# Two transformer layers with experts: dense pieces placed between and behind double score steps, and another order of pieces between layer 0's attention and the experts

## The chip, the cores and the metric

The kernel runs on one core of one Trainium2 chip. The metric is the time of one execution in device microseconds, lower is better; it is given as the median of repeated runs. All engines of the core work side by side: TensorE (PE in the profile, with its weight loads as PEld), VectorE (DVE), ScalarE (ACT), GpSimd (POOL) and SyncE (SP, which here only issues DMAs). Each engine runs its own instructions in the order in which the program wrote them, and waits on semaphores for the others.

## The reference

The input is `x` of 8 images, 1024 tokens, 256 features, all in fp32. Four blocks follow each other, each on the layer norm of `x` and added to `x`:

```python
x = x + _L0_attn_ref(_layernorm(x), ...)   # 16 heads of 16, a window of 128 tokens to each side
x = x + _L0_ffn_ref(_layernorm(x), ...)    # 8 experts, the best 2 per token, and a shared expert
x = x + _L1_attn_ref(_layernorm(x), ...)   # 16 heads, blocks of 64: own band, first and last block
x = x + _L1_ffn_ref(_layernorm(x), ...)    # one product with a ternary weight, and a bias
```

In layer 0's feed-forward each token goes through the two experts with the largest logits, weighed by a softmax of the two, and through the shared expert. An expert is `silu(x @ wg.T) * (x @ wu.T) @ w_down.T` with 384 hidden features. In layer 1's attention the first and the last block of 64 queries see all 1024 keys; the others see the first and the last block and the three around them.

## The kernel before

The program has three stretches: layer 0's attention over images 0 to 7, the experts over groups of 256 or 128 gathered tokens, and layer 1's attention over images 0 to 7. What else has to be done (norms, projections, routing, the shared expert, the last product) is cut into small **pieces** that are put beside the attention.

**Steps.** `attention` (used by both layers) walks through steps. A step writes, in this order: `weights` (the products of keys and queries for one pack of key tiles, 4 heads side by side in 4 PSUM banks, line 459; ScalarE takes the exponential of each bank, line 466, and in layer 0 POOL cuts the window's edge out of it, line 915); `sums` of the pack of two steps ago (line 489, all into one bank); one call of `scores` (the same products the other way round, four banks, line 404; VectorE takes each bank's row maximum, lines 422, 427 and 431); whatever is `later` (transposes of maxima, line 442, or of a finished sum, line 504); and then pieces. Scores run ahead of weights, since the maximum is put into the queries before the weights are made. There are 7 PSUM banks for all of this but the sums. Layer 0 has 24 steps for an image and 32 score rounds, layer 1 has 28 steps and 36 rounds. So some steps call `scores` twice, the **double steps**: in layer 1 those are steps 2, 6, 9, 13, 16, 20, 23 and 27 of an image. In such a step pieces can stand between the two calls and behind the second.

```python
if some:
    fill_until(step + 0.5)
    scores(*some.pop(0))
fill_until(step + 1)
```

**Due times.** `beside` holds, for each image, lists of pieces with due times in steps, counted from the image's step 0. `fill_until(time)` runs all pieces that are due before `time`, the earliest first. So a piece with a due time of 9.3 stands between the two calls of step 9, one of 9.8 behind them. A list given with one start and one end time spreads its pieces over that time by their weights. Times of 28 and more fall in the next image's steps. `need` can draw a piece forward when something requires it.

**Pieces of layer 1.** For image b: `qk_pieces` (eight products for queries and keys, two matmuls each on TensorE at line 282, then activations on ScalarE, lines 302 and 314), the first four heads' pairs as `first` in the image before, the others in the image's own steps; `values` (two matmuls, line 338, and a VectorE add, in `v_pieces`); `gather` (an indirect DMA by POOL) and `add` for the experts' outputs; `stats`, `scaled` (norm; `scaled` also holds the transposes, line 235). For image b-1, which has just left the attention: `stats`, `scaled`, `biased` (POOL), and eight `product` pieces (line 1324: two matmuls, a VectorE add, and a store on SP after every second one).

**Pieces at the end of layer 0.** When attention works on image 7, it has beside it the projection, norm and routing of image 6. `route_pieces` are `logits`, `by_token`, two `best` (VectorE's top 8), `mine`, `counts` (two matmuls at line 721 that wait for `mine`, then some 14 small VectorE operations) and `weighed`; after them come 16 `scatter` pieces, each a small POOL copy and an indirect DMA (lines 742 and 751) that put rows in their experts' buckets in DRAM. Behind image 7's attention stands one `chain` of pieces, in a fixed order: image 7's projection (line 878, after transposes at line 867), norm, routing and scatter; the tables that say which expert each group belongs to (`ranges`, `rests`, `offsets`, `groups`, all on VectorE, and `by_group`, line 1114, a matmul with VectorE behind it); and the shared expert of image 6, cut into 12 `up` pieces (8 matmuls in the profile's count at line 611, a tanh at line 617, two VectorE operations at lines 622 and 623) and 4 `down` pieces (line 631, with an add at line 795). `some(n)` takes the next n pieces of the shared expert. Two `up` pieces can be taken in two parts, `shared_in_two`: the matmuls and the tanh, and later the VectorE part, `gated`.

**The experts.** `experts` loads for each group the rows (`xs`, line 1160, only after the last scatters) and the expert's weights (lines 1172 and 1174) by tables that `by_group` made: SP reads `which` and `where` and issues the loads.

Of the kernel before, what the change touches and what calls it, by code (L numbers as in the profile page):

```python
# [19 lines left out]
B, S, D = 8, 1024, 256  # L20
# [30 lines left out]
def seq_kernel(  # L51
# [135 lines left out]
    def piece(weight, f, *args, first=(), then=None):  # L187
        return weight, lambda: f(*args), first, then
# [582 lines left out]
    shared_in_two = {}  # L771
# [35 lines left out]
    def layer0():  # L807
# [42 lines left out]
        def before_it(b):  # L850
            qk_of[b], xnT_of[b] = {}, []
            norm = norm_pieces(b, "xnT", xnT_of[b], "xnT")
            first = qk_pieces(b, 0, 0, wq_sb, wk_sb, xnT_of[b], qk_of[b])
            values = v_pieces(b, 0, wv_sb, xnT_of[b])
            return norm, first, [
                piece(0.1, biased, b, jp, first=[("xnT", b, 3)]) for jp in range(4)
            ], values
# [84 lines left out]
        for b in range(B + 1):  # L942
            lists = []
            if b == 0:
                (stats, scaled), first, biases, values = before_it(0)
                lists.append((-1, -1e-6, (
                    stats + scaled[:2] + [piece(0.0, f) for f in (clear_maxima, masks)] + scaled[2:]
                    + first + [piece(0.0, ones_in_v, 0)] + values + biases
                )))
                lists.append((1, 2, [piece(0.0, clear_bucket), piece(0.0, ones_in_v, 1)]))  # L950
            if b > 0:
                half0, half1, (stats, scaled), route, scatter, shared = after_it(b - 1)
            if b < B:


                lists.append((
                    0, [4.7, 5.3, 5.8, 6.6],
                    qk_pieces(b, 1, 0, wq_sb, wk_sb, xnT_of[b], qk_of[b]),
                ))
                if b > 0:  # L960
                    lists.append((0, [-0.1, -0.05, 0.6, 1.6], half0))
                    lists.append((0, [2.7, 2.75, 3.5, 4.3], half1))
                    lists.append((0, [3.1, 4.1, 4.8, 7.2], stats))
                    lists.append((0, [6.1, 6.8, 8.85, 10.2, 10.7], scaled))
                    if b + 1 < B:
                        lists.append((0, [11.7, 12.5, 13.6, 15.5, 16.3, 16.8, 18.1], route))
                        lists.append((0, [17 + 0.8 * i for i in range(STREAMS)], scatter))
                    else:
                        lists.append((11.3, 14, route))
                        lists.append((14, 20.5, scatter[:10]))  # L970
                    late = scatter[10:]
            if b == B:

                def some(n):
                    return [rest.pop(0) for _ in range(n)]

                ranges, rests, offsets, groups, by_group = tables()
                lists.append((0, [0.1] * 6, late))

                lists.append((0, [1.1] * 2 + [2.05] * 3, half0[:3] + stats[:1] + half0[3:]))  # L980
                two = [shared_in_two[B - 2](*x) for x in ((0, 2), (1, 0))]
                chain = (
                    stats[1:2] + half1[:3] + scaled[:1] + stats[2:3] + half1[3:] + stats[3:]
                    + scaled[1:2] + some(1) + scaled[2:3] + some(1) + scaled[3:] + route[:5]
                    + [x[0] for x in two] + route[5:6] + scatter[:4] + [x[1] for x in two]
                )
                some(2)
                chain += (
                    some(1) + [ranges] + some(1) + [rests] + some(1) + [offsets] + some(1)
                    + [groups] + some(3) + [by_group] + scatter[4:] + route[6:] + rest  # L990
                )
                lists.append((2.1, 8, chain))
                left_over.extend(shared)
            elif b + 1 < B:


                if b > 0:
                    lists.append((
                        0, [7.6, 8.3, 8.7, 9.6, 10.6, 11.3, 11.8, 12.6, 13.5, 14.3, 14.8, 15.6]
                        + [20.3, 23.4, 26.3, 26.8, 26.85], shared,  # L1000
                    ))
                (stats, scaled), first, biases, values = before_it(b + 1)
                lists.append((0, [2.9 if b > 1 else 0.0], [piece(0.0, load, b + 1)]))
                lists.append((0, [7.8, 9.8, 12.1, 12.8], stats))
                lists.append((0, [13.1, 13.8, 15.1, 15.8, 16.2], scaled))
                lists.append((0, [16.7, 17.3, 17.8, 18.6], first))
                lists.append((0, [19.5, 20.8, 21.6, 22.6], values))
                lists.append((0, [18.5, 20.5, 21.8, 23.5], biases))
            else:

                rest = shared
            beside.append(lists)
# [216 lines left out]
    def layer1():  # L1229
# [174 lines left out]
        for b in range(B + 1):  # L1404
            lists = []
            if b == 0:
                (gather, add), (stats, scaled), first, values = before_it(0)

                rest = [piece(x[0], x[1]) for x in left_over]

                def some(n):
                    return [rest.pop(0) for _ in range(n)]

                begun = gather[:]
                for j, n in enumerate((3, 2, 1, 2, 1, 2, 1, 1)):
                    begun += some(n) + add[j : j + 1] + (stats[j // 2 : j // 2 + 1] if j % 2 else [])
                for x in scaled:
                    begun += [x] + (some(1) if len(rest) > 1 else [])
                lists.append((-1, -1e-6, begun + first + rest))
                lists.append((-0.95, -0.1, values))  # L1420
            if b < B:
                lists.append((
                    0, [0.4, 1.4, 2.2, 3.3, 4.4, 5.4, 6.2, 7.6],
                    qk_pieces(b, 1, 1, wq_sb, wk_sb, xnT_of[b], qk_of[b]),
                ))
            if b == B:
                (stats, scaled), biases, products = after_it(b - 1)
                scaled, turned = scaled[:4], scaled[4:]
                lists.append((
                    0, [-1.9, -0.9, -0.8, -0.7, 0.9, 0.92, 0.94, 0.96, 1.8, 1.9] + [2.5] * 14,  # L1430
                    stats[:2] + scaled[:2] + turned[:1] + biases[:1] + turned[1:2] + biases[1:2]
                    + products[:4] + stats[2:] + scaled[2:] + turned[2:] + biases[2:] + products[4:],
                ))
            elif b > 0:
                (stats, scaled), biases, products = after_it(b - 1)
                lists.append((0, [1.6, 2.8, 4.6, 5.5], stats))
                lists.append((0, [5.7, 7.4, 8.4, 10.3, 11.3], scaled))
                lists.append((0, [7.9, 8.8, 10.9, 11.8], biases))
                lists.append((0, [9.7, 10.5, 11.4, 12.6, 13.2, 13.8, 14.6, 15.6], products))
            if b + 1 < B:  # L1440
                gathered, (stats, scaled), first, values = before_it(b + 1)
                if b == 0:
                    lists.extend(combining(
                        gathered, 1.5, [0.5 + 0.4 * i for i in range(16)],
                        [3.5, 4.5, 5.5, 6.8, 7.5, 8.5, 9.5, 10.3], b + 1,
                    ))

                lists.append((0, [5.6, 7.6, 10.4, 10.7] if b == 0 else [-7.1, -3.6, 0.6, 10.6], stats))
                lists.append((0, [11.5, 12.4, 14.4, 15.4, 16.4], scaled))
                lists.append((0, [16.8, 17.3, 17.7, 18.4, 19.4, 20.2, 20.7, 21.3], first))  # L1450
                lists.append((0, [19.8, 21.7, 22.3, 23.2, 24.2, 25.3, 26.3, 27.2], values))
            if b + 2 < B:
                lists.extend(combining(
                    gathers(b + 2), 16.2, [12 + 0.6 * i for i in range(16)],
                    [18.6, 19.6, 21.4, 22.5, 24.7, 25.5, 26.5, 28.3], b + 2,
                ))
            if b + 3 < B:
                lists.append((0, [3.9], [piece(0.0, placed, b + 3)]))
            beside.append(lists)
# [8 lines left out]
    with ExitStack() as ctx0:  # L1468
        layer0()
    with ExitStack() as ctx1:  # L1470
        layer1()
# [76 lines left out]
```

## Time and profile before

| what | value |
|---|---|
| median of 3 runs | 3046.15 us (3043.94 to 3050.73) |
| profiled execution | 3047.95 us |
| its span | 3046.2 us |
| mean granted TensorE clock | 0.991 |
| layer 0's attention, of the span | up to about 1167 us |
| between it and the experts' first product | about 1167 to 1235 us |
| experts | about 1235 to 1825 us |
| layer 1, one image in the middle | 146.0 us |

All durations below come from the one profiled execution. Each line of a timeline has the start in us, the time from the first start to the last end, the engine, the line of the kernel, the operation, what it writes and reads, its shape and how many instructions were merged; behind them in brackets the idle time before and what ended it. TensorE's matmuls overlap, so the time that a group costs is read from its start to the next group's start. TensorE counts as busy while a matmul that has been issued waits; such a wait shows only as a group that takes longer than the same group elsewhere. In waits, a line gives the engine and line that waited, whom it waited for, the total, the number of waits and the longest.

### The profile page before, as it was taken

The page shows a single profiled execution, that of the slowest core. Times are in us where ns is not written, and L with a number is a line of the kernel's source. Part 1 is how long each engine was busy: PE and PEld are TensorE (multiplying, and loading weights), DVE is VectorE, ACT ScalarE, POOL GpSimd, SP SyncE. Part 2 cuts the span into 40 slices and gives each one's busy share as a digit, 9 for nine tenths or more (in the row PEclk, how much of TensorE's full clock was granted, in tenths as well). Part 3 has the DMA queues.
Part 4 walks back from the last instruction along what each step waited for, and adds up shares of the span by engine and source line. Part 5 has one row for each costly group of instructions (what it writes and reads, how often), then busy time and mean ns, then how long its engine had stood idle before and what let it go on. Part 6 is the DMA issues. An engine that isn't in the chain of part 4 may idle for free. (4 is left out here: it accounts for less than half of the span.)

```text
span 3046.2 us, 81036 instructions
## 1 busy us (share of the span) xinstructions
PE 2967.0 (97%) x32684; PEld 1907.1 (63%) x32684; DVE 1896.5 (62%) x5996; ACT 1389.0 (46%) x2845; POOL 994.3 (33%) x2406
## 2 busy tenths in 40 slices
PE   8999999999999998999999998999999999999998
PEld 4455555555555545788888885555555555555554
DVE  5667676666667665344333345776767686767564
ACT  4454454444444442122222213555556555656554
POOL 4334454545453546000000011424242434243223
PEclk9999999999999999999999998999999999999998
DMA  3000101010101001666666642101010101010000
GB/s 107 2 2 16 42 17 41 19 39 19 40 22 36 24 26 46 217 208 213 230 211 213 213 147 62 35 9 52 7 57 2 57 2 57 6 54 6 12 13 19
DMA packets 109447, 198.18 MB, mean 65 GB/s; under 512 B 11152, under 2 KB 81296, under 8 KB 109072
## 3 DMA queue, kind: packets, MB, share of 16 engines
q1 hardware_dynamic: 96784, 159.43, 15.7%
q0 software_dynamic: 12288, 33.57, 3.5%
q8 instruction: 257, 4.21, 0.6%
q14 instruction: 118, 0.97, 0.1%
HBM read 139.22 MB, written 53.74 MB: 63 GB/s over the span
## 5 line engine op out<-in xcount | busy, mean ns | idle before, releaser
L466 ACT ACTIVATE w<-pst 128x512 f32<-128x512 f32 (+1 forms) x1664 | 834.7, 589 | 581.6 <-PE pst L459 560.4
L915 POOL TENSOR_SCALAR_AFFINE_SELECT w<-w 128x256 f32<-128x256 f32 x896 | 335.4, 406 | 525.1 <-ACT w L466 523.8
L427 DVE TENSOR_REDUCE maxima<-pst 128x1 f32<-128x320 f32 (+1 forms) x896 | 368.2, 473 | 215.2 <-PE pst L404 175.9
L422 DVE CUSTOM_DVE_ANT_0 junk<-pst,mask_mid 128x320 f32<-128x320 f32 x768 | 330.6, 486 | 181.1 <-PE pst L404 177.3
L489 PE MATMUL pso<-w,v 128*32 128x256 f32 (+5 forms) x6400 | 434.7, 388 | 2.1 <-ACT oT L498 2.1
L617 ACT ACTIVATE th<-pst 128x256 f32<-128x256 f32 (+1 forms) x309 | 117.0, 379 | 654.2 <-PE pst L611 622.6
L611 PE MATMUL pst<-xsT,of 128*128 128x256 f32 (+1 forms) x1704 | 383.6, 375 | 0.8 <-ACT xsT L1186 0.7
L611 PEld LDWEIGHTS pst<-xsT,of 128*128 128x128 f32 x1704 | 313.1, 191 | 40.4 <-ACT xsT L1186 0.9
L1354 POOL MEMSET w<- 64x128 f32 x768 | 151.8, 199 | 557.6 <-ACT w L466 531.5
L1283 POOL DMA_INDIRECT y<-made,from x128 | 122.2, 955 | 620.0 <-DVE h L622 587.4
L622 DVE SCALAR_TENSOR_TENSOR h<-th,pst 128x256 f32<-128x256 f32 (+1 forms) x309 | 128.2, 415 | 289.1 <-ACT th L617 281.5
L489 PEld LDWEIGHTS pso<-w,v 128*32 128x32 f32 x6400 | 157.9, 109 | 216.4 <-issue 154.8
L431 DVE TENSOR_REDUCE two<-pst 128x1 f32<-128x512 f32 x256 | 159.0, 684 | 114.1 <-PE pst L404 84.2
L631 PE MATMUL pst<-of,h 128*128 128x256 f32 x828 | 190.5, 379 | 0.0
L631 PEld LDWEIGHTS pst<-of,h 128*128 128x128 f32 x828 | 157.0, 190 | 21.2
L623 DVE TENSOR_TENSOR h<-h,pst 128x256 f32<-128x256 f32 (+1 forms) x309 | 128.3, 415 | 10.6
L211 POOL TENSOR_TENSOR rstd<-var,neg_half 128x4 f32<-128x4 f32 x64 | 67.3, 1052 | 186.8 <-DVE var L210 132.4
L1366 POOL TENSOR_TENSOR x<-x,ao 64x64 f32<-64x64 f32 (+1 forms) x192 | 78.6, 416 | 104.1 <-DVE ao L597 86.2
L206 DVE BATCH_NORM_STATS2 stats<-x 128x6 f32<-128x256 f32 x256 | 103.9, 406 | 1.2 <-POOL x L1366 0.9
L631 PE MATMUL pst<-shared_down,h 128*128 128x256 f32 x384 | 94.4, 395 | 8.6 <-issue 4.9
L1194 DVE COPY ys<-pst 128x512 f32<-128x512 f32 (+1 forms) x71 | 48.0, 676 | 84.6 <-PE pst L631 84.5
L422 DVE CUSTOM_DVE_ANT_0 junk<-pst,mask_last 128x256 f32<-128x256 f32 x128 | 46.7, 421 | 72.9 <-PE pst L404 72.9
(831 smaller groups left out, 4886.0 us busy)
## 6 DMA issues: line engine op xcount, KB each, us to landing
of<-in_w_up_dram SPq DMA_DIRECT2D x71, 768.0 KB, 4.9
of<-in_w_down_dram SPq DMA_DIRECT2D x71, 384.0 KB
xs<-bucket SPq DMA_DIRECT2D x67, 256.0 KB, 6.2
made<-ys SPq DMA_DIRECT2D x67, 256.0 KB, 2.1
x<-in_x_dram SPq DMA_DIRECT2D x32, 256.0 KB, 3.9
between<-x SPq DMA_DIRECT2D x8, 1024.0 KB
x<-between SPq DMA_DIRECT2D x32, 256.0 KB, 3.9
out_dram<-x SPq DMA_DIRECT2D x24, 256.0 KB, 3.1
```

What stands on the lines that cost most here:

```text
L422: nc.vector.tensor_tensor_reduce(out=junk[:, 0:many], in0=ps[:, 0:many], in1=mask, scale=-1.0, scalar=3e38, op0=ALU.add, op1=ALU.min, accu ...
L427: nc.vector.tensor_reduce(to[:, r, :], ps[:, 0:many], AX.X, ALU.max, negate=True)
L431: nc.vector.tensor_reduce(twos[0][:, r, n : n + 1], ps[:, 0:many], AX.X, ALU.max, negate=True)
L466: nc.scalar.activation(w[:, r, 0:n], ps[r][:, 0:n], AF.Exp)
L489: nc.tensor.matmul(columns(po[rows[r], :], to - 512 * half, many, step), lhsT=v_of[b % 2][:, kt, head : head + 32], rhs=w[:, r, n : n + many],
L611: nc.tensor.matmul(ps[:, part * GT : part * GT + n], lhsT=up_sb[:, kc, f0 : f0 + 128], rhs=xT[:, kc, :], start=(kc == 0), stop=(kc == 1),)
L622: nc.vector.scalar_tensor_tensor(h, th, 1.0, g, ALU.add, ALU.mult)
L623: nc.vector.tensor_tensor(h, h, u, ALU.mult)
L631: nc.tensor.matmul(ps[:, t * D : (t + 1) * D], lhsT=hs[fc][:, t * 128 : (t + 1) * 128], rhs=down_sb[:, fc, :], start=(fc == 0), stop=(fc = ...
L915: nc.gpsimd.affine_select(out=part, in_=part, compare_op=ALU.is_ge, fill=0.0, base=0, pattern=[[0, 2], [sign, 128]], channel_multiplier=-sign,
L1283: nc.gpsimd.indirect_dma_start(out=y, out_offset=None, in_=made[:, :], in_offset=bass.IndirectOffsetOnAxis(ap=place[b][:, n, j : j + 1], a ...
L1354: nc.gpsimd.memset(part, 0.0)
```

## The change

Only due times and the order of pieces change; no piece is added, removed or rewritten.

In layer 0, beside the attention of image 7, the routing of image 6 gets due times of its own (before: spread from 11.3 to 14), with `counts` at 15.2 instead of 13.4, and its first ten scatters are spread from 15.4 to 21.4 instead of from 14 to 20.5. In the chain behind the attention, two more `up` pieces stand ahead of image 7's routing, other two `up` pieces are taken in two parts, the first `down` stands ahead of their `gated`, and fewer pieces of the shared expert stand between the later tables.

In layer 1, query and key pieces move from steps 1 and 7 to steps 2 and 6, one `scaled` from step 8 to 7 with two `biased`, the first three `product` pieces to steps 9, 9 and 10, and all `values` pieces to later times, the last one into step 1 of the next image.

```diff
                     else:
-                        lists.append((11.3, 14, route))
-                        lists.append((14, 20.5, scatter[:10]))
+                        lists.append((0, [11.6, 12.5, 12.9, 13.4, 13.8, 15.2, 15.7], route))
+                        lists.append((15.4, 21.4, scatter[:10]))
...
-                two = [shared_in_two[B - 2](*x) for x in ((0, 2), (1, 0))]
+                two = [shared_in_two[B - 2](*x) for x in ((1, 1), (1, 2))]
                 chain = (
-                    stats[1:2] + half1[:3] + scaled[:1] + stats[2:3] + half1[3:] + stats[3:]
-                    + scaled[1:2] + some(1) + scaled[2:3] + some(1) + scaled[3:] + route[:5]
-                    + [x[0] for x in two] + route[5:6] + scatter[:4] + [x[1] for x in two]
+                    stats[1:2] + half1[:2] + some(1) + half1[2:3] + scaled[:1] + stats[2:3]
+                    + half1[3:] + stats[3:] + scaled[1:2] + some(1) + scaled[2:3] + some(1)
+                    + scaled[3:4] + some(1) + scaled[4:] + route[:5] + [x[0] for x in two]
+                    + route[5:6] + scatter[:4] + some(1) + [x[1] for x in two]
                 )
                 some(2)
                 chain += (
-                    some(1) + [ranges] + some(1) + [rests] + some(1) + [offsets] + some(1)
-                    + [groups] + some(3) + [by_group] + scatter[4:] + route[6:] + rest
+                    [ranges] + some(1) + [rests] + some(1) + [offsets] + some(1) + [groups]
+                    + some(2) + [by_group] + scatter[4:] + route[6:] + rest
                 )
...
                 lists.append((
-                    0, [0.4, 1.4, 2.2, 3.3, 4.4, 5.4, 6.2, 7.6],
+                    0, [0.4, 2.2, 2.8, 3.4, 4.4, 5.4, 6.2, 6.8],
                     qk_pieces(b, 1, 1, wq_sb, wk_sb, xnT_of[b], qk_of[b]),
                 ))
...
                 lists.append((0, [1.6, 2.8, 4.6, 5.5], stats))
-                lists.append((0, [5.7, 7.4, 8.4, 10.3, 11.3], scaled))
-                lists.append((0, [7.9, 8.8, 10.9, 11.8], biases))
-                lists.append((0, [9.7, 10.5, 11.4, 12.6, 13.2, 13.8, 14.6, 15.6], products))
+                lists.append((0, [5.7, 7.4, 7.9, 10.3, 11.3], scaled))
+                lists.append((0, [7.6, 8.4, 10.9, 11.8], biases))
+                lists.append((0, [9.3, 9.8, 10.6, 12.6, 13.2, 13.8, 14.6, 15.6], products))
...
-                lists.append((0, [16.8, 17.3, 17.7, 18.4, 19.4, 20.2, 20.7, 21.3], first))
-                lists.append((0, [19.8, 21.7, 22.3, 23.2, 24.2, 25.3, 26.3, 27.2], values))
+                lists.append((0, [16.8, 17.3, 17.8, 18.4, 19.4, 20.2, 20.8, 21.4], first))
+                lists.append((0, [22.4, 23.2, 23.8, 24.6, 26.6, 27.2, 27.8, 29.4], values))
```

## The prediction

> **What bounds the kernel now.** I read the page first. TensorE is the bound: it is busy for 97% of the span.
>
> ```profile
> PE 2967.0 (97%) x32684; PEld 1907.1 (63%) x32684; DVE 1896.5 (62%) x5996; ACT 1389.0 (46%) x2845; POOL 994.3 (33%) x2406
> ```
>
> So the change can only win idle time, half-clock time, or waits that lie inside the "busy" time. Next come TensorE's waits between 1090 and 1215 us, where layer 0's attention ends and the experts are prepared.
>
> ```profile
> PE pst L721 <- DVE sofar L727: 4.0, 2, 3.4
> PE pst L631 <- DVE h L623: 2.8, 1, 2.8
> PE pst L235 <- DVE rows__15310 L223: 2.4, 2, 1.4
> PE pst L878 <- ACT aoT L872: 2.0, 1, 2.0
> ```
>
> L721 is `counts`: one call waits 3.36 us. The table by stretches shows what follows a starved stretch. The columns are the stretch's length, the busy time of PE, PEld, DVE, ACT and POOL, the granted clock, and DMA.
>
> ```profile
> 1122.80:1126.20 3.40, 0.23 (x3) 0.00 (x0) 3.26 (x21) 0.70 (x2) 1.56 (x5) 1.00 0.00 0
> 1126.20:1133.10 6.90, 6.72 (x48) 3.28 (x48) 3.83 (x22) 1.73 (x5) 1.27 (x4) 0.51 0.01 4
> 1194.50:1197.90 3.40, 1.08 (x6) 0.63 (x5) 2.79 (x15) 0.00 (x0) 0.30 (x2) 1.00 0.00 0
> 1197.90:1201.30 3.40, 2.95 (x7) 2.41 (x8) 1.15 (x3) 0.00 (x0) 1.25 (x2) 0.50 0.11 39
> ```
>
> After the 3.36 us wait TensorE runs 6.9 us at half clock; after the 2.77 us wait, 3.4 us. A wait costs more than its length.
>
> Last, TensorE's timeline in layer 1. I take times from start to start, since the ends are modelled. The first six lines are the ends of double steps 6, 23 and 27 of one image, with nothing behind the second scores (L404), and the next step's weights (L459 x8). The last three are double step 13 of image 7, with a dense piece (L1324) behind.
>
> ```profile
> 2348.55 1.09 PE L404 MATMUL pst<-k__26876,q__26874 32*64 32x128 f32 x32
> ...
> 2349.57 2.04 PE L459 MATMUL pst<-q__26874,k__26876 32*128 32x512 f32 x8
> ...
> 2442.48 0.80 PE L404 MATMUL pst<-k__29042,q__29040 32*64 32x128 f32 x32
> 2443.21 2.23 PE L459 MATMUL pst<-q__27743,k__27745 32*128 32x512 f32 x8
> ...
> 2461.13 1.09 PE L404 MATMUL pst<-k__29042,q__29040 32*64 32x128 f32 x32
> 2462.15 2.37 PE L459 MATMUL pst<-q__29040,k__29042 32*128 32x512 f32 x8
> ...
> 2961.35 1.09 PE L404 MATMUL pst<-k__36319,q__36317 32*64 32x128 f32 x32
> 2962.37 1.13 PE L1324 MATMUL pst<-wt_sb,xnT__36840 128*128 128x256 f32 x4
> 2963.43 1.64 PE L459 MATMUL pst<-q__36317,k__36319 32*128 32x512 f32 x8
> ```
>
> The same eight matmuls take 1.97 us (2349.57 to 2351.53) after step 6, 2.16 after step 23, 2.30 after step 27, but 1.57 with the piece behind and 1.09 at the shortest (2403.70). They wait for a bank that VectorE's maxima still hold; the page calls that busy. Such waits recur in each 146 us image.
>
> **Layer 0.** The sum is made against the profiled execution's 3047.95 us.
>
> *`counts` of image 6.* It moves from step 13 (right behind two `best`, `mine`) to step 15. VectorE's pile that it waits for (busy from 1119.08 to 1126.3) is worked off in the two steps between, so 3.36 us of wait and half of 6.9 us go: -6.8. VectorE's 2.8 us of `counts` and 0.9 of `weighed` then fall between maxima; three steps (1134.12 to 1147.93, 13.8 us) hold some 8.4 us of VectorE work (16 maxima at 0.44 from start to start, 0.69 and 0.67), so a bank may be late: +0.8 (0 to 2.0). The first scatter now follows `counts` in the same step and waits on POOL for `to`, with step 16's affine selects behind it; their readers come two steps later, and POOL idled 7.5 us before 1131.83, so 0.
>
> *Its ten scatters* (a row copy of 0.2 us and a DMA_INDIRECT of 1.0 each, 1.37 per pair with the gap) move past the selects: two now land in step 20 instead of step 19. POOL works without a gap from there:
>
> ```profile
> 1158.49 0.98 POOL L751 DMA_INDIRECT bucket<-rows__14188,torow  x1 [0.16 <-issue]
> 1159.48 6.54 POOL L915 TENSOR_SCALAR_AFFINE_SELECT w<-w 128x256 f32<-128x256 f32 x18
> ```
>
> The last 14 of these 18 selects start 2.7 us later, and the last sums wait for them. The least is 0, if selects were early; the most 2.7 and a half-clock stretch of 1.7. I take +2.5, because the last sums begin at 1165.36 and the selects end at 1166.02.
>
> *Before the last `counts`* two more up pieces (8 matmuls, 1.72 us each by L611; a tanh and two DVE of 0.42) are run. They fill the 1.96 us at L878 and the 1.36 us at the fourth `rows__15310`; the 1.00, 0.46 and 0.67 us waits stay, as VectorE sets them. 3.44 - 1.96 - 1.36 gives +0.1, and the xnT copy behind a tanh 0.3: +0.4 (0 to 0.8).
>
> *Behind it.* `down` goes ahead of the two `gated`, so the 2.77 us at L631 and its 1.7 of half clock go from TensorE. But VectorE's chain from `counts` (1194.7) to `spread` holds, by its rows in the new order (`counts`, an add of `down`, two `gated`, ranges, `gated`, rests, an add, offsets, `gated`, groups), 2.8 + 0.7 + 1.7 + 2.7 + 0.8 + 0.7 + 0.7 + 2.8 + 0.8 + 2.7 = 16.4 us, against TensorE's 12.3 (two downs of 2.7, four ups of 1.72): a new wait of about 4 us at L1114. It costs nothing while another chain is longer: the last 16 scatters run on POOL from 1197.58 to 1221.38 and their packets land by 1222.5, and the experts' first rows are loaded only then. In the trace the rows were issued at 1227.23, since SP's loads behind `which` began at 1221.70, and landed at 1233.46 beside two experts' weights. Now `which` comes near 1213, the weights are issued early, the rows at about 1223.5, and land in 3.9 to 6.2 us (page, part 6): 3.7 to 6 us earlier. Against that, TensorE's signals were up to 7 us late here (matmuls ended at 1213.0, tanh at 1220.02); if this stays, the gain is 0. I take -4.0 (-6 to 0). The 4 to 6 us idle before the experts puts up to one more stretch at half clock behind it: +0.8 (0 to 1.7).
>
> The page TensorE: Matmul & The Clock Gate of the Trainium skill (Why this matters for your kernels) asks for no idle gaps over about 3 us; here a gap of 2.77 us was followed by half clock, so the row decides. By the rule that gap would cost 1.7 less.
>
> Sum: -6.8 + 0.8 + 2.5 + 0.4 - 4.0 + 0.8 = -6.3, between -13 and +2.
>
> **Layer 1, per image.** Five pieces of two products (0.96 us, 1.06 where a copy trails) leave single steps and are put at doubles, which then have one between and one behind (steps 2, 6, 9, 23, 27; 13, 16 and 20 keep theirs). Query and key pieces bring ACT work; `product` and `values` a DVE add of 0.42; `product` 1 its store on SP, where nothing is late.
>
> Added, each at 1.06 less what the next x8 weights give back. Step 6: 1.97 becomes the 1.57 of the last fence, +0.66. Step 27: 2.30 becomes 1.57, +0.33. After doubles of kind 2, 9, 16, 23 a piece behind gave 1.49 (2364.95) and 1.09 (2403.70); I take 1.3. Step 2 (1.75 now): +0.6. Step 23 (2.16): +0.3 with 0.1 for the second scores. Step 9 gets its piece between: by step 16, which has a transpose there, 4.8 us instead of 4.34, +0.4. The last `values` is due at 29.4, the next image's step 1, ahead of the sums of step 30 that would draw it forward: its add comes at 2327.05 to 2327.47 by VectorE's queue, and the sums that read it start at 2327.25: +0.2. Together +2.5. At best the waits swallow all (+0.5); at worst nothing (+5.3).
>
> Taken away, each at 0.96 less the wait that comes to light at the next weights. The nearest rows are image 7's bare steps: x24 takes 1.55 (2985.42) with only the maxima's transposes ahead, against 1.22 after step 25 now: -0.5. Step 21: x24 1.39 becomes 1.48 (2968.11): -0.8. Step 19 keeps transposes and a key piece, as step 5, whose next weights show no wait: -1.0. Step 11: x24 1.09 becomes x16's 1.50 (2358.88): -0.55. Steps 7 and 8 (a piece leaves; a transpose moves from 8 to 7): -0.5. Together -3.35 (-4.8 if no wait comes to light, -2.3 if each bares 0.5).
>
> Net -0.87 an image for images 1 to 6. Image 0 has no products before it and nothing in its step 1: -1.4; image 7 has no `values` to make: +0.7. That is -6 in all. All best ends together would be -4.3 an image, all worst +3.0; some two thirds of the way, -3 and +2, give -21 and +14.
>
> The skill's page Trainium Kernel Development and Optimization (Best Practices) says to mind PSUM pressure: packed matmuls speed up compute, not evacuation. It speaks against this half: a piece behind takes a bank itself. By it alone the wait would move, not shrink, the worst end above; the 1.57 against 1.97 to 2.30 says that about half goes.
>
> Total: -12.3, so 3035.65 by the profiled execution, whose time lies 1.8 above the median: 3034.
>
> **The rivals.** All start from 3046.15; a measurement tells a difference from none at about 0.2%, 6 us.
>
> *The waits swallow the pieces whole:* -3 an image is some -20 in layer 1, and with layer 0's -6 that is 3020. For it: step 16, where x8 has no wait left at 1.09. Against: 1.57 after step 13.
>
> *Only `counts` counts:* late signals hold the experts' start, layer 1 gains nothing: -3, 3043. For it: tanh at 1220.02.
>
> *VectorE sets the pace in layer 1 (slower):* it is busy 105.4 of 146 us, over 90% in some steps. If each added piece costs its 1.06 in full (+5.3 instead of +2.5), an image takes 1.9 us more: +14, with layer 0's -6 some 3054. It decides from +0.9 an image (no gain left), and from +1.8 the kernel is slower by 0.2%. Against: the 1.57 after step 13.
>
> **How the numbers follow.** Likeliest, as summed, 0.5 (3026 to 3040 by itself); the waits swallow all 0.17; only `counts` 0.20; VectorE 0.13. Faster gets 0.49 + 0.17 + 0.07 = 0.73; slower 0.11; within 0.2% the rest. 3017 to 3049 leaves out some 0.05 below and 0.14 above.
>
> **What would show it.** Right: no wait at `counts` of image 6 and full clock after it; a new wait of about 4 us at L1114; the first rows 4 us earlier after `counts`; x8 weights behind doubles at 1.1 to 1.6 us and images of 145 us. Wrong: a longer wait for the last sums than 3 us, x24 weights over 1.6 us after bare steps, or images over 147 us.

## The result: slower, by 0.4%

The changed kernel takes 3060.66 us, the median of 6 runs (3053.80 to 3063.30), against 3045.05 us before (6 runs, 3043.26 to 3050.73) on the same chip: a ratio of 1.004, with a 95% interval of 1.0025 to 1.0055. The forecast was 3034 us and "faster". The profiled execution took 3059.23 us, with a span of 3057.5 us, 11.3 us more than before.

In the listings of the changed kernel, and of every version with the new chain, lines behind the chain are numbered one higher than before: L1325 is `product`, L1115 `by_group`. On the profile's page TensorE's busy time has hardly moved:

```profile
PE 2968.1 (97%) x32684; PEld 1900.7 (62%) x32684; DVE 1895.2 (62%) x5996; ACT 1387.3 (45%) x2845; POOL 994.7 (33%) x2406
```

The waits of TensorE say where the time went. First the longest line of the kernel before, which the forecast did not show (total, number of waits, longest):

```profile
PE pst L235 <- DVE xn L223: 25.5, 9, 9.7
```

and the same view of the changed kernel:

```profile
PE pst L235 <- DVE xn L223: 42.9, 16, 9.2
...
PE pst L1115 <- DVE spread L1106: 4.1, 1, 4.1
...
PE pst L721 <- DVE sofar L727: 3.2, 6, 0.5
```

The 3.36 us wait at `counts` (L721) is gone, and `by_group` waits 4.1 us, as forecast. But the transposes of layer 1's `scaled` (L235) wait seven times more, 17.4 us in all. Here is one of the seven, in TensorE's timeline:

```profile
2352.06 1.13 PE L282 MATMUL pst<-xnT__26517,wk_sb 128*128 128x256 f32 x4
2353.12 1.31 PE L459 MATMUL pst<-q__26874,k__26876 32*128 32x512 f32 x8
2354.37 1.08 PE L489 MATMUL pso<-w,v 128*32 128x256 f32 x24
2355.37 1.11 PE L404 MATMUL pst<-k__26876,q__26874 32*64 32x512 f32 x16
2356.42 0.66 PE L235 MATMUL pst<-ident,xn 128*128 128x128 f32 x4
2359.69 1.09 PE L235 MATMUL pst<-ident,xn 128*128 128x128 f32 x4 [2.62 <-DVE xn L223]
2360.71 2.09 PE L459 MATMUL pst<-q__26874,k__26876 32*128 32x128 f32 x24
```

and VectorE's timeline over the same stretch:

```profile
2356.54 2.48 DVE L431 TENSOR_REDUCE two<-pst 128x1 f32<-128x512 f32 x4 [2.62 <-PE pst L404]
2359.06 0.16 DVE L435 TENSOR_REDUCE maxima<-two 128x4 f32<-128x8 f32 x1
2359.14 1.37 DVE L223 TENSOR_SCALAR xn<-x,mv,rstd 128x256 f32<-128x256 f32 x4
```

A `scaled` piece holds the transposes of the previous pair and VectorE's subtraction for its own pair (its result is `xn`). In step 7 the scores are issued first, then two `scaled` pieces with nothing on TensorE between them. The first issues the subtraction on VectorE behind the four maxima of the step's own scores (2.48 us and 0.16); the second transposes that subtraction's result at once. TensorE stands still for 2.62 us, and the table by stretches (length, busy time of PE, PEld, DVE, ACT and POOL, granted clock, DMA) shows what follows:

```profile
2355.80:2359.20 3.40, 1.27 (x20) 0.42 (x4) 2.62 (x6) 1.19 (x3) 0.00 (x0) 1.00 0.00 0
2359.30:2362.60 3.30, 2.91 (x28) 2.37 (x28) 1.21 (x4) 0.58 (x1) 0.00 (x0) 0.50 0.00 0
```

The pieces behind the double steps did what the forecast said: the weights behind step 6 take 1.25 us (2353.12 to 2354.37) instead of 1.97. Steps in us, from start to start of their weights, mean of images 1 to 5 (the third row is explained below):

| steps | 2, 3 | 6 | 7 | 8 | 9, 10 | 11, 12 | 19 to 22 | 23, 24 | 25, 26 | 27, 0 | image |
|---|---|---|---|---|---|---|---|---|---|---|---|
| before | 9.68 | 5.21 | 5.47 | 3.84 | 10.75 | 9.52 | 22.96 | 9.93 | 8.77 | 10.62 | 146.03 |
| after | 10.08 | 6.27 | 7.39 | 4.98 | 11.11 | 9.08 | 19.85 | 10.34 | 8.42 | 11.55 | 148.59 |
| after, xn early | 10.08 | 6.47 | 4.31 | 3.83 | 11.12 | 9.08 | 19.63 | 10.33 | 8.42 | 11.54 | 144.19 |

### The profile page after: what moved, and what is told of

Its sections match the earlier page's. It is cut to its first block, busy times and chain, and to the rows that moved or that the text cites. A ratio compares the mean times of both kernels' runs of the same rounds, so it can differ in the third digit from the quotient of the medians.

```text
span 3057.5 us, 81031 instructions
## 1 busy us (share of the span) xinstructions
PE 2968.1 (97%) x32684; PEld 1900.7 (62%) x32684; DVE 1895.2 (62%) x5996; ACT 1387.3 (45%) x2845; POOL 994.7 (33%) x2406
## 5 line engine op out<-in xcount | busy, mean ns | idle before, releaser
L466 ACT ACTIVATE w<-pst 128x512 f32<-128x512 f32 (+1 forms) x1664 | 833.4, 589 | 595.8 <-PE pst L459 572.3
L631 PEld LDWEIGHTS pst<-of,h 128*128 128x128 f32 x828 | 157.0, 190 | 21.2
L211 POOL TENSOR_TENSOR rstd<-var,neg_half 128x4 f32<-128x4 f32 x64 | 66.7, 1042 | 188.8 <-DVE var L210 164.2
L235 PE MATMUL pst<-ident,xn 128*128 128x128 f32 x384 | 65.2, 297 | 42.9 <-DVE xn L223 42.9
```

The costliest lines, as they stand in the source:

```text
L466: nc.scalar.activation(w[:, r, 0:n], ps[r][:, 0:n], AF.Exp)
L631: nc.tensor.matmul(ps[:, t * D : (t + 1) * D], lhsT=hs[fc][:, t * 128 : (t + 1) * 128], rhs=down_sb[:, fc, :], start=(fc == 0), stop=(fc = ...
```

## The experiments

All ratios are to runs of the kernel before on the same chip, with 95% intervals.

### The two halves apart

The kernel before with layer 0's edits alone, and with layer 1's alone.

> The kernel before with the change's layer 0 alone (the lists of image 7's predecessor and the chain ahead of the experts). Theory: the stretch came out about as forecast in the changed kernel's trace (second xs transposes 5.5 us earlier once an offset of 1.1 that lies before the change is taken off): 3038 to 3041, -4 to -7 us. Rival (layer 0's gain depends on the chance of the clock's windows, or is taken back by late signals): 3043 to 3047.

> The kernel before with the change's layer 1 alone. Theory: the whole loss lies here, +18 us by the images' lengths in the two traces: 3060 to 3067, with the seven waits at L235 for `xn` of 2.2 to 2.6 us and half clock behind each. Rival (the two halves disturb each other, for instance by the place of the clock's windows): under 3056.

Layer 0 alone: 0.9985 (0.9973 to 0.9997), 3046.87 us against 3049.24, a gain of some 4.6 us by the ratio. Layer 1 alone: 1.0041 (1.0026 to 1.0056), 3062.85 us, with the seven waits (44.0 us in 16 waits). The loss is layer 1's. The halves would multiply to 1.0026 against the 1.004 of the whole, which the intervals allow.

### The suspected step undone, and alone

```diff
-                lists.append((0, [5.7, 7.4, 7.9, 10.3, 11.3], scaled))
-                lists.append((0, [7.6, 8.4, 10.9, 11.8], biases))
+                lists.append((0, [5.7, 7.4, 8.4, 10.3, 11.3], scaled))
+                lists.append((0, [7.9, 8.8, 10.9, 11.8], biases))
```

> The changed kernel, with only layer 1's pieces of `scaled` and `biases` back at their old places (the second `scaled` in step 8 again). Theory (the lost cover): in the changed kernel the second `scaled` of step 7 waits 2.2 to 2.6 us for VectorE's xn behind four maxima and a stretch at half clock follows, which makes steps 7 and 8 longer by 1.91 + 1.13 = 3.04 us an image where -0.5 was forecast; undone, that is 3.5 us an image in seven images, some -25 us: 3033 to 3038, the wait at L235 for `xn` back from 16 to 9 waits, no half clock in images 1 to 6, images of about 145 us. Rival (VectorE sets the pace, each added piece costs its price in full, wherever it stands): one piece moved back gives at most its own transposes' wait, -0.5 an image: 3055 to 3060, and images stay at 147 or more.

3035.29 us, ratio 0.9944 (0.9927 to 0.9960): this one edit turns a loss of 0.4% into a gain of 0.6%. The waits at L235 are back to 9 (25.1 us), and the images without a stretch at half clock take 144.1 to 144.2 us. The other way round, the kernel before with this move alone:

> The kernel before with only the move of layer 1's second `scaled` (8.4 to 7.9) and of two `biases`; the last query or key piece stays at 7.6, between the two `scaled`. Theory (the step of the forecast that failed, alone): as in the run with that piece in between, the second `scaled` waits about 1.7 us for VectorE's xn behind four maxima, with a stretch at half clock in some images: +1.5 to +2 an image, 10 to 14 us slower than before. Rival (it takes the other moves of layer 1 to make the loss): within 4 us of before.

3063.29 us, ratio 1.0066 (1.0050 to 1.0082): the move loses by itself, and the rival falls. The loss is larger than expected (15 to 25 us by the interval). Its trace, with a span 15.2 us longer than that of before, shows 148.0 us an image instead of 146.0, 13.9 us over all eight. Steps 7 and 8 take 11.30 us instead of 9.31, with full clock in step 8 of images 1 to 6: the move costs 2 us an image even where no half clock follows. Part of what the median has beyond the trace lies in the comparison: the profiled execution of the kernel before took 3047.95 us, 3.5 us more than the median of its runs here (3044.48). The rest stays unexplained.

### What the transposes wait for

Three things changed around the wait: the second `scaled` came nearer, a key piece left step 7, and the dense pieces sit elsewhere. This run leaves TensorE's order as in the changed kernel, instruction by instruction, and only lets VectorE make the second `xn` earlier, by issuing the subtraction and the transposes as pieces of their own. The third `xn` moves too, to a step later; on VectorE it stands behind the second, so it can't be what the second's transposes wait for:

```diff
-                tiles=tile_at, apart=b == B - 1,
+                tiles=tile_at, apart=True,
...
-                lists.append((0, [5.7, 7.4, 7.9, 10.3, 11.3], scaled))
+                lists.append((0, [5.7, 5.72, 8.0, 10.4], scaled[:4]))
+                lists.append((0, [7.4, 7.9, 10.3, 11.3], scaled[4:]))
```

> The changed kernel with TensorE's, ScalarE's and GpSimd's work for a step as it is; only VectorE's two subtractions for the second `scaled` of layer 1 are issued with the first one's, ahead of the four maxima of double step 6's second scores, instead of behind them, and the third's a step later. Theory (the second `scaled` waits for VectorE's xn behind the maxima): the wait at L235 and the half clock behind it go, 2.5 + 1.1 us in each of seven images, while the maxima and so a bank come up to 0.7 us late: some -20 to -25 us against the changed kernel, 11 to 17 us faster than before, images of 144 to 146 us, the wait at L235 for `xn` back to 9 times. Rival (step 7 has too many banks in use, or the two transposes stand too close whatever VectorE does): the wait takes another name and images stay over 147, less than 6 us gained on the changed kernel.

3033.14 us, ratio 0.9938 (0.9925 to 0.9951). TensorE's timeline of this run, the same step:

```profile
2339.77 1.31 PE L459 MATMUL pst<-q__26874,k__26876 32*128 32x512 f32 x8
2341.02 1.08 PE L489 MATMUL pso<-w,v 128*32 128x256 f32 x24
2342.02 1.11 PE L404 MATMUL pst<-k__26876,q__26874 32*64 32x512 f32 x16
2343.07 1.09 PE L235 MATMUL pst<-ident,xn 128*128 128x128 f32 x8
2344.09 1.59 PE L459 MATMUL pst<-q__26874,k__26876 32*128 32x128 f32 x24
```

The eight transposes run without a gap. So it is shown that the place of these subtractions, two VectorE instructions each, in VectorE's own queue made the loss: 148.59 us an image against 144.19, with the same TensorE program. (The expectation calls the maxima double step 6's; the timeline above shows that those waited for are of step 7's own scores. In this run the subtraction passes them and the eight of step 6.) The rival of the forecast, a VectorE that sets the pace, falls with it: VectorE stood idle for 2.62 us right before those maxima.

The last run of this group puts work into the gap instead:

```diff
-                    0, [0.4, 2.2, 2.8, 3.4, 4.4, 5.4, 6.2, 6.8],
+                    0, [0.4, 2.2, 2.8, 3.4, 4.4, 5.4, 6.2, 7.6],
```

> The changed kernel with one edit: the last query or key piece of layer 1 back from 6.8 (behind double step 6) to 7.6, so that it stands between the two `scaled` of step 7 as cover. Theory (the lost cover): VectorE makes the second `xn` at the same time, TensorE has 1.06 us of work in the gap, so the wait falls from 2.6 to about 1.5 us, step 6 gets shorter by 0.7 and the half clock behind goes (1.1): -1.8 an image, -12 us in seven: 3046 to 3051. If the wait falls but the half clock stays, -5: 3054 to 3057. Rival (VectorE sets the pace): the piece costs the same at either place, 3058 to 3062, and the wait only changes its name.

3048.35 us, ratio 0.9994 (0.9984 to 1.0004). The wait falls to 1.75 us in each image. Images 2, 3 and 5 take 146.0 to 146.3 us, images 1 and 4 147.5 to 147.6: there, and in image 6, half clock followed. Its table by stretches around the wait, for an image with half clock and one without:

```profile
2499.10:2502.50 3.40, 1.65 (x19) 1.05 (x21) 3.10 (x8) 1.72 (x4) 0.00 (x0) 1.00 0.00 0
2502.60:2505.90 3.30, 3.30 (x48) 1.75 (x48) 0.00 (x0) 2.30 (x6) 0.86 (x5) 0.50 0.02 5
2349.00:2352.40 3.40, 3.40 (x50) 1.46 (x48) 1.11 (x4) 2.16 (x4) 0.00 (x0) 1.00 0.03 5
2352.50:2355.80 3.30, 1.55 (x11) 1.07 (x9) 3.27 (x9) 1.60 (x3) 0.00 (x0) 1.00 0.00 0
```

The same wait, about the same busy time, and another clock behind it: step 8 takes 4.96 us in the first image and 3.40 in the second. A stretch at half clock costs 1.56 us here; what decides whether it comes is not shown.

### Where layer 1's gain comes from

The kernel before with the `values` moved and nothing else:

```diff
-                lists.append((0, [19.8, 21.7, 22.3, 23.2, 24.2, 25.3, 26.3, 27.2], values))
+                lists.append((0, [22.4, 23.2, 23.8, 24.6, 26.6, 27.2, 27.8, 29.4], values))
```

> The kernel before with only layer 1's `values` moved (from 19.8 .. 27.2 to 22.4 .. 29.4). Theory (by the steps of the runs with the old `scaled`, steps 19 to 0 hold nearly all of layer 1's gain: -0.80 - 0.82 - 1.77 + 0.06 + 1.06 - 0.66 - 0.67 + 0.30 + 1.66 - 0.73 = -2.4 an image): -2.4 an image less up to 1.1 for the last piece, which now shares step 1 with a key piece: -1.3 to -2.4 in each of six images, 8 to 14 us faster than before. Rival (the gain is from the pieces put behind doubles in general, as forecast): -0.5 an image, 3 us.

3035.65 us, ratio 0.9961 (0.9947 to 0.9975), images of 144.2 us. One list holds what layer 1 has to win. By the steps, most of it is in 19 to 22: in the kernel before, the second scores of double step 20 take 2.02 us and the weights of step 21 another 2.02; with the `values` gone from step 19 and 21 they take 1.18 and 1.08. First the kernel before, from the second scores of step 20 to the weights of step 21:

```profile
2424.59 0.43 PE L404 MATMUL pst<-k__27745,q__27743 32*64 32x128 f32 x4
2425.40 0.43 PE L404 MATMUL pst<-k__27745,q__27743 32*64 32x128 f32 x2 [0.38 <-DVE two L431]
2426.00 0.68 PE L404 MATMUL pst<-k__27745,q__27743 32*64 32x128 f32 x26 [0.17 <-DVE two L431]
2426.61 1.13 PE L282 MATMUL pst<-xnT__28684,wq_sb 128*128 128x256 f32 x4
2427.67 2.09 PE L459 MATMUL pst<-q__27743,k__27745 32*128 32x512 f32 x8
2429.69 1.07 PE L489 MATMUL pso<-w,v 128*32 128x256 f32 x24
```

and this run:

```profile
2420.86 1.08 PE L404 MATMUL pst<-k__27741,q__27739 32*64 32x128 f32 x32
2422.04 1.13 PE L282 MATMUL pst<-xnT__28684,wq_sb 128*128 128x256 f32 x4
2423.10 1.14 PE L459 MATMUL pst<-q__27739,k__27741 32*128 32x512 f32 x8
2424.18 1.08 PE L489 MATMUL pso<-w,v 128*32 128x256 f32 x24
```

The trace shows that these waits go; whether VectorE's add in front of that double step (0.42 us) alone made them wasn't tried.

### Layer 0: the lists and the chain

> The kernel before with only the lists of the last image but one (routing earlier or later by steps, ten scatters from 15.4 to 21.4). Theory: the gain at `counts` is given back: 0 (-2 to +2) against before; in the trace steps 15 to 18 take 17.6 us instead of 13.8, and the stretch from step 18 to the first projection is 1.8 longer. Rival (the forecast): -3.5, with the three steps at 14.6.

> The kernel before with only the new order of the chain ahead of the experts. Theory: all of layer 0's gain is here, -3 to -6 against before; the first projection stands where it stood, the last `counts` comes 0.6 earlier, and from there to the experts' first transposes it takes 34 to 35 us instead of 39, with a wait of 4.1 us at L1114. Rival (late signals hold the start): 0.

The lists alone: 1.0003 (0.9995 to 1.0012). The chain alone: 0.9983 (0.9974 to 0.9991). So all of layer 0's gain is the chain's, and the lists, forecast at -3.5 us, are worth nothing. From step 13 to 15 the lists do gain: 14.8 us becomes 9.4. But steps 15 to 18 take 17.7 us instead of 13.8. The changed kernel's timelines show why, first ScalarE's and then TensorE's:

```profile
1139.09 0.21 ACT L710 ACTIVATE ex<-ex 128x8 f32<-128x8 f32 x1 [4.86 <-DVE ex L709]
1139.21 2.04 ACT L466 ACTIVATE w<-pst 128x512 f32<-128x512 f32 x4
```

```profile
1137.06 0.75 PE L404 MATMUL pst<-k__14041,q__14039 32*64 32x320 f32 x4
1138.01 0.72 PE L404 MATMUL pst<-k__14041,q__14039 32*64 32x320 f32 x2 [0.20 <-DVE rank L732]
1139.84 0.78 PE L404 MATMUL pst<-k__14041,q__14039 32*64 32x320 f32 x10 [1.10 <-ACT w L466]
```

`weighed` has one small exponential on ScalarE (L710) between two runs of VectorE work. It needs a subtraction that stands behind `counts` on VectorE, so ScalarE waits 4.86 us, and four exponentials of the weights (L466) wait behind it, though TensorE has made what they read; until they are done, their banks are not free. A stretch at half clock follows (1140.70 to 1144.10). The test moves `weighed` away and leaves TensorE's order as it is:

```diff
-                        lists.append((0, [11.6, 12.5, 12.9, 13.4, 13.8, 15.2, 15.7], route))
+                        lists.append((0, [11.6, 12.5, 12.9, 13.4, 13.8, 15.2, 17.5], route))
```

> The kernel before with the lists of the last image but one as changed, but `weighed` at 17.5 instead of 15.7. Theory (ScalarE runs `weighed`'s exponential, which waits for VectorE behind `counts`, in front of four exponentials of the weights, so TensorE waits 1.1 us for a bank and a stretch at half clock of 1.7 follows): both go, steps 15 to 18 take 14 to 15 us instead of 17.6, and the kernel is 2 to 4 us faster than before, where the lists alone were not. Rival (the bank waits for the maxima behind VectorE's 2.8 us of `counts`, whatever ScalarE does): the steps stay above 16.5 us and the time stays at before's.

1.0002 (0.9988 to 1.0016). The mechanism is right, and no gain clear of the noise comes of it: steps 15 to 18 take 14.0 us, the wait and the half clock are gone, but from step 18 to the first projection it now takes 24.6 us (before 21.0, with the lists alone 22.8). Counted from step 13 and against the kernel before, this trace is 5.2 us ahead at step 18, 1.7 at the first projection, 3.4 at the last `counts`, and only 0.6 at the experts' first transposes. The end of GpSimd's timeline of this run:

```profile
1160.55 0.19 POOL L742 COPY torow<-to 128x1 uint32<-128x1 uint32 x1
1160.90 0.98 POOL L751 DMA_INDIRECT bucket<-rows__14188,torow  x1 [0.16 <-POOL torow L742]
1161.89 5.06 POOL L915 TENSOR_SCALAR_AFFINE_SELECT w<-w 128x256 f32<-128x256 f32 x14
```

The last 14 selects end at 1166.95, and GpSimd has no gap longer than 0.2 us from 1145 on: TensorE comes earlier to the tail and waits there for GpSimd. Two runs took layer 1's early xn and `weighed` at 17.5 together, the second with four of the ten scatters moved behind the attention:

```diff
-                        lists.append((15.4, 21.4, scatter[:10]))
-                    late = scatter[10:]
+                        lists.append((15.4, 21.4, scatter[:6]))
+                    late = scatter[6:]
...
-                lists.append((0, [0.1] * 6, late))
+                lists.append((0, [0.1] * 10, late))
```

> The changed kernel with the second `scaled`'s xn made early in layer 1 and `weighed` of the last image but one moved from 15.7 to 17.5, away from `counts`. Theory: as with the early xn alone (18 us faster than before) and 2.5 to 3.5 us more: 18 to 24 us faster than before. Rival (the loss at `counts` comes from the maxima behind VectorE's pile, not from `weighed`): no more than the early xn alone, 16 to 20 us.

> The changed kernel with the early xn, `weighed` at 17.5, and four of the ten scatters that run in the tail of layer 0's attention put behind it with the other six. TensorE's order is the same as without this edit. Theory (with the wait at `counts` and the one behind `weighed` gone, GpSimd sets the end of the attention: no gap from 1145 to 1167 us, selects behind scatters): four pairs of 1.37 us fewer ahead of the last selects, the last sums' wait of 1.36 us and the half clock beside it go, and from step 18 to the first projection it takes 21 to 22 us instead of 24.5: some 3 us, 17 to 23 us faster than before in all. Rival (TensorE's and ScalarE's own chain sets the tail): 24 us as without the edit, 14 to 18 us faster.

Without the edit: 3028.50 us, 0.9950 (0.9931 to 0.9970). That is some 15 us faster than before (9 to 21), where 18 to 24 were expected, and no better than the early xn alone (0.9938); so it is not shown that the move of `weighed` adds anything. With the edit: 3027.84 us, 0.9944 (0.9928 to 0.9959), some 17 us faster (13 to 22), which fits both its theory and its rival. In the traces the edit does what was expected of the tail: from step 18 to the first projection 21.2 us instead of 24.6, so GpSimd's queue was the bound. And the gain is lost once more: the first projection comes 3.4 us earlier, the last `counts` 1.4 us later than without the edit. GpSimd makes the norm's `rstd` (L211), which stands right behind the moved scatters and comes 1.15 us later than without the edit. But VectorE, which makes the normed rows, has another input that comes later still. GpSimd's and VectorE's timelines of the run with the edit:

```profile
1173.97 1.05 POOL L211 TENSOR_TENSOR rstd<-var,neg_half 128x4 f32<-128x4 f32 x1
1175.53 0.42 DVE L622 SCALAR_TENSOR_TENSOR h<-th,pst 128x256 f32<-128x256 f32 x1 [5.44 <-ACT th L617]
1176.92 0.73 DVE L223 TENSOR_SCALAR rows__15320<-x,mv,rstd 128x256 f32<-128x256 f32 x2
```

`rstd` is done at 1175.02; the rows start at 1176.92, behind work that waited for ScalarE's tanh until 1175.53. So the tanh of the `up` piece ahead of the rows came last, and why it is late isn't settled. TensorE then waits 2.53 us for the first normed rows and 1.30 for the second; without the edit it waited 0 and 1.00.

### Two more versions

> The kernel before with layer 0's new chain ahead of the experts and layer 1's edits except those of `scaled` and `biases`; the lists for the last image but one (routing and ten scatters) stay as before. Theory (the lists gain 5.4 us at `counts`, give back 3.8 in the next three steps and 1.8 in the tail, so they are worth nothing): the same as with the lists, 13 to 19 us faster than before. Rival (the forecast: the lists are worth -3.5): 10 to 14 us faster than before.

> Layer 0 of the changed kernel with `weighed` at 17.5; in layer 1 only `values` and the query and key pieces' 1.4 and 3.3 (to 2.2 .. 3.4) moved, while the last query or key piece stays at 7.6 and `scaled`, `biases` and `products` stay as before. Theory: the moves of `values` and of the key piece of step 1 are all that wins in layer 1 (-2.4 + 0.4 an image, -13 in all), layer 0 gives -5 to -8: 17 to 22 us faster than before, as fast as any version so far. Rival (the moves of `products` and the last key piece win as well): 2 to 5 us less than the version with all of them and the early xn.

The first (new chain, old lists, layer 1 without the move of `scaled`): 3030.91 us, 0.9934 (0.9919 to 0.9948), some 20 us faster than before (16 to 25); the rival's 10 to 14 lie outside. The second (`values` and one key piece moved in layer 1, layer 0 with `weighed` at 17.5): 3029.54 us, 0.9950 (0.9931 to 0.9969), some 15 us (9 to 21), a little less than expected. Its images 1 to 5 take 143.94 us, against 143.93 to 144.25 in the three versions with the early xn; so in the traces the moves of `products` and of the last key piece win nothing, though the times alone could not exclude the rival's 2 to 5 us. All of these versions beat the kernel before by 0.5 to 0.7%; their intervals overlap, so no order among them is claimed.

## Why the prediction was wrong

**The step that failed** is "Steps 7 and 8 (a piece leaves; a transpose moves from 8 to 7): -0.5". Measured, steps 7 and 8 take 12.37 us instead of 9.31: +3.06, so 3.56 an image off, some 25 us over the seven images that have it. Forecast and result are 26.7 us apart. The forecast asked what the moved transposes cost TensorE. It did not ask where their operand comes from, and when: that `scaled`'s subtraction is issued by the piece just before, in the same step, behind four maxima of 2.48 us. The two due times, 7.4 and 7.9, show it: both pieces fall behind the one call of scores of step 7. In the kernel before a key piece and then the weights, sums and scores of step 8 stood between the two pairs of transposes (4.8 us in its trace, 2353.59 to 2358.35). And the key piece, the last cover left, was moved away by the same change; with it left in place the wait is still 1.75 us.

**Layer 1's other terms** came out near or better, but for step 27. Two of them were not what their own rule gives: 0.96 less the bared wait is -0.63 for step 25 (1.55 against 1.22) and -0.87 for step 21 (1.48 against 1.39), where -0.5 and -0.8 were written. Per image, forecast and measured (after): steps 2 and 3 +0.6, +0.40; step 9 +0.4, +0.36 with step 10; step 11 -0.55, -0.44 with step 12; steps 19 and 21 -1.8, -3.11 for 19 to 22; step 23 +0.3, +0.41 with step 24; step 25 -0.5, -0.35 with step 26; step 27 +0.33, +0.93 with the next step 0; the last `values` +0.2, 0.00. The weights behind doubles with a piece behind took 1.25 (step 6), 1.49 (23; 2448.09 to 2449.58) and 1.58 us (27; 2467.66 to 2469.24), forecast 1.57, 1.3 and 1.57. TensorE's timeline of the changed kernel at steps 23 and 27:

```profile
2448.09 1.56 PE L459 MATMUL pst<-q__27739,k__27741 32*128 32x512 f32 x8
2449.58 0.64 PE L489 MATMUL pso<-w,v 128*32 128x128 f32 x12
...
2467.66 1.64 PE L459 MATMUL pst<-q__29040,k__29042 32*128 32x512 f32 x8
```

With the early xn, steps 6 to 8 together come to +0.09, where +0.66 and -0.5 made +0.16, and an image gains 1.84 us, forecast 0.87; the surplus is the wait in steps 20 and 21: the forecast expected a longer wait once the pieces had left, and there the wait went with them.

**Layer 0** went the forecast way in sum, but not in its parts. Traces start this stretch (step 13) up to 2.6 us apart, so differences between two points of one trace count. Forecast and measured (after):

| part | forecast | measured |
|---|---|---|
| wait and half clock at `counts` (steps 13 to 15) | -6.8 | -5.4 |
| "so a bank may be late" (steps 15 to 18) | +0.8 | +3.8 |
| ten scatters (step 18 to the first projection) | +2.5 | +1.8 |
| first projection to the last `counts` | +0.4 | -0.5 |
| `counts` to the experts' first transposes | -4.0 + 0.8 | -4.6 |
| sum | -6.3 | -4.9 |

The residue behind `counts` was mis-sized at 0 to 2.0, since it counted VectorE's maxima and not ScalarE's queue behind `weighed`. "Their readers come two steps later ... so 0" for GpSimd was wrong too: in the trace of the lists alone GpSimd waits 3.98 us for `to` with six selects behind it, and later it sets the tail's end. In the chain the size was right: `by_group` waits as forecast (below), the first rows are there earlier, and 39.5 us from the last `counts` to the first transposes became 34.9. The gain came another way than forecast, though. The rows were to be issued some 4 us earlier, since the weights' loads ahead of them on SP would be early. SP issued them 32.2 us behind `counts`; it was 33.2 before, and the forecast's 1223.5 would have been 29.5. SP now waits for the last scatters' data. But the rows land sooner once issued: the first transposes start 2.7 us behind the issue instead of 6.3. Why they do wasn't tried. First the kernel before, then the changed one:

```profile
1227.23 1.62 SPq L1160 DMA_DIRECT2D xs<-bucket  x2
1233.50 0.66 PE L1181 MATMUL pst<-ident,xs 128*128 128x128 f32 x4 [1.62 <-DMA xs<-bucket]
```

```profile
SPq L1161 <- DMA bucket<-rows__15320,torow: 2.9, 2, 1.8
1227.47 0.39 SPq L1161 DMA_DIRECT2D xs<-bucket  x1
1230.15 0.66 PE L1182 MATMUL pst<-ident,xs 128*128 128x128 f32 x4 [1.12 <-DMA xs<-bucket]
```

These are `by_group` and the next `down` in the changed kernel:

```profile
1212.26 0.74 PE L1115 MATMUL pst<-spread,ones 128*128 128x142 f32 x2 [4.11 <-DVE spread L1106]
1224.82 4.22 PE L631 MATMUL pst<-shared_down,h 128*128 128x256 f32 x10 [3.89 <-DVE h L623]
```

The 3.89 us wait at the next `down` was not forecast; it lies beside the wait for the experts' rows, for which TensorE still waits 1.12 us behind it.

**The rivals.** "VectorE sets the pace" had the right sign and, by chance, nearly the right time (3054). Its mechanism was refuted: the added pieces did not cost their price in full, and VectorE was idle where TensorE waited. "The waits swallow the pieces whole" asked for -3 us an image; without the step that failed it is -1.84, and steps 27 and 0 alone cost +0.93. "Only `counts` counts" fails on both sides: layer 1 has those 1.84 us, and the lists that hold `counts` are worth nothing. The case that came true was none of those listed, and the result lies 11.7 us above the range. It would have been found by asking for each moved piece which engine makes its input, and what stands in front of that on its queue.

## What to carry to other kernels

When a piece is moved on the busiest engine, follow its inputs too: find the instruction that makes each, on whatever engine, and read what stands ahead of it in that engine's order; an engine that is idle half the time can still be too late. Where a piece both uses the last one's result and makes the next one's, two of them need as much other work between them as the making and what stands ahead of it take (a key piece between them still left a wait of 1.75 us), or the making has to be issued a step ahead. And a gain ahead of a queue that is full can end as a longer wait at the end of that queue (here GpSimd's selects behind scatters took back 3.5 of 5.2 us).

## What the runs showed of the hardware

- At the wait at L235 the half clock followed a stretch, not a gap. In these traces a time at one clock is always a multiple of 3.41 us long. In four of the traces with the wait at L235 (28 images), I took the 3.41 us stretch of that grid in which TensorE was busy least: where it was busy for 0.39 or less, half clock followed in 11 of 11; from 0.47 to just under 0.50 in 4 of 10; at 0.50 and more in 0 of 7. So the same 1.75 us wait, at 0.49 in both images shown above, led to half clock once and not the other time, and the 2.62 us wait escaped it where a border of the grid cut it in two (busy 0.56). The Trainium skill's page TensorE: Matmul & The Clock Gate (Why this matters for your kernels) warns of idle gaps over about 3 us. Here 1.75 us could be enough. These limits hold for this place alone. Elsewhere in the changed kernel half clock also followed stretches in which TensorE was busy for more by the records: 0.62 (1137.3 to 1140.7), 0.77 (2263.7 to 2267.1) and 0.84 (1867.8 to 1871.2). Matmuls that have been issued and wait count as busy there, so the records can't tell how much of it was work.
- A single 0.21 us instruction on ScalarE, whose input was late, held up 2.04 us of ready work behind it and so cost TensorE 1.10 us and a stretch at half clock.
